# Layer 3 of a four-layer convolution net: two kinds of products move to GpSimd, a Gelu buffer changes its tag, and spectra move between pixel tiles

## The chip, the core and the metric

The kernel runs on one core of a Trainium2 chip. The core has TensorE (PE, matmuls; its weight loads are listed apart as PEld), VectorE (DVE), ScalarE (ACT), GpSimd (POOL) and SyncE (SP, which here only issues DMAs). The metric is the device time of the whole program in microseconds, as the median of several runs.

## The reference

The input is 4 images of 48 channels and 256 x 256 pixels, all in float32. Four layers follow each other, each as `x = x + layer(groupnorm(x))`. The first is a gated convolution with an 8 x 8 Fourier filter, the second and third are scans over rows and columns with five-wide convolutions. Only the fourth, layer 3, is touched:

```python
y = jnp.einsum('oc,bchw->bohw', w_in, x)                  # 48 -> 288 channels
yp = y.reshape(B, C2, ht, P, wt, P).transpose(0, 1, 2, 4, 3, 5)   # 8 x 8 patches
f = jnp.fft.rfft2(yp) * fft_mask[None]
yp = jnp.fft.irfft2(f, s=(P, P))
y = yp.transpose(0, 1, 2, 4, 3, 5).reshape(B, C2, H2, W2)
y = lax.conv_general_dilated(y, w_dw, ..., feature_group_count=C2)   # 3 x 3, per channel
x1, x2 = jnp.split(y, 2, axis=1)
g = jax.nn.gelu(x1, approximate=False) * x2
return jnp.einsum('oc,bchw->bohw', w_out, g)              # 144 -> 48
```

## The kernel before

**Tiles and steps.** Layer 3 works on pairs of images, a and b, in strips of 8 rows (RB = 8). There are two pairs, each with 32 strips and a tail step for the last row, so 66 steps. A strip is first normalised (`normed`, ACT), transposed (`turned`, PE), taken to the spectrum (`waves`, PE), multiplied by w_in (`spectrum`: matmuls `pz` on L1093, then the Fourier mask on VectorE, L1096 into `z` and L1101 into `zr`), and taken back to pixels (`pixels`: matmuls `pp` on L1131, copies on L1051 by ACT or VectorE into `z_a` or `z_b`).

**The 3 x 3 convolution.** The 288 channels are split: 2 x 128 wide ones (half 0 goes through the Gelu, half 1 is the other factor) and 2 x 16 last ones. It is done in four ways:

- image a, all 8 rows: nine taps as diagonal matmuls on PE (`taps`, L1171), units `a0` and `a1` of a step
- image b, lower 4 rows: the same on PE (`lower_taps`, L1187), unit `b`; its gate is L1197 (ACT) and L1199 (VectorE, `g_b`)
- image b, upper 4 rows: `begin` makes tap 0 on ACT (L1230) and the other eight on VectorE (L1235), for half 0 and then half 1. After tap 8 of half 0 comes the Gelu (L1237, ACT); after tap 8 of half 1 the product of both halves (L1239), in place in `whole[step]`
- the last 16 + 16 channels of both images: `narrow` makes each tap as an ACT product `part` (L1261) and a GpSimd sum (L1262) into `acc_m`, in two halves of 512 elements. Then `narrow_gate` takes the Gelu (L1280, ACT) into a buffer `curved[0]` and makes four products of 32 partitions x 512 elements (L1283), two for each j0.

The result is put together in `mixed`: matmuls with w_out, first of the product `whole` (L1298), then of `g_a`, `g_b` and `acc_m` (L1310, acc_m last); VectorE adds the residual into `xo` (L1322) and SyncE writes it out (L1329).

**Order.** PE, DVE, ACT and SP run in the order in which the program is written (`manual_schedule`); GpSimd's order is made by a scheduler. A step has three stages, in each of which `together` runs nine rounds of two PE units and mixes other work in: `3n` with unit a0, `3n + 1` with a1, `3n + 2` with b. VectorE's taps of image b wait in the queue `due`; `together` takes one in certain rounds: 0, 1, 3, 4, 6, and in every third stage in round 7 too. So half 1's taps 1 to 5 fall in stage 3n + 2, taps 6 to 8 and the product in the next stage 3n, then half 0's taps. The sums of the last channels wait in `coming` and are taken by `product`. `gate_few` calls `narrow_gate` in rounds 4 and 6 of stage 3n, and `store` (with `mixed`) follows in stage 3n + 1, after the copies of a1's pixels (L1051 on VectorE).

**Buffers.** All matmul results share one PSUM tag "w" with four buffers, so each new `pp`, `pz`, `pd` or `po` takes the place of the fourth before it and waits for its readers. In SBUF the pool `io` has two buffers per tag: `gl` (Gelu results of 1024 elements: units a0, lower_gate, and curved[0]) and `xo` (residual sums).

**Before stage 3n + 2** stands, word for word:

```python
                wave(n + 1, "AA")
                product()
                lower(n, 1, 0, "AA")
                product()
                lower(n, 1, 8, "AA")
                product()
                spectra(n + 1, 0)
```

`lower(n, 1, q0, ...)` makes half 1's pixels of image b in two tiles of eight patches' width (q0 = 0 and 8) and calls `begin` after the second. `spectra(n + 1, 0)` makes the next step's spectrum of half 0 in four parts, each with its own PSUM buffer, a group of matmuls (L1093) and one VectorE instruction (L1096).

Of the kernel before, what the change touches and what calls it, by code (L numbers as in the profile page):

```python
# [9 lines left out]
F32 = mybir.dt.float32  # L10
AF = mybir.ActivationFunctionType
ALU = mybir.AluOpType
# [21 lines left out]
class Net:  # L34
# [901 lines left out]
    def layer3(self, x, scs):  # L936
# [6 lines left out]
        nc, tc, W, H, NQ, HD = self.nc, self.tc, self.W, self.H, self.NQ, HID3  # L943
# [4 lines left out]
        with ExitStack() as st:  # L948
            pool = lambda name, bufs, **k: st.enter_context(tc.tile_pool(name=name, bufs=bufs, **k))
            wp, inp, wz = pool("w3", 1), pool("in3", 1), pool("z3", 1)  # L950
            io, mid = pool("io3", 2), pool("mid3", 1)
            ps_w = pool("ps3w", 4, space=PSUM)
            st.enter_context(tc.manual_schedule(engines=FIXED | {mybir.EngineType.SP}))
            HR = RB // 2
# [129 lines left out]
            def spectrum(xf, k, q0, n):  # L1084

                m = NM if k == 0 else NM + 2 * NR
                pz = ps_w.tile([128, 2, MM], F32, name="pz", tag="w")[:, :, 0 : n * m].rearrange(
                    "p b (q c) -> p b q c", c=m
                )
                for q in range(n):  # L1090
                    for b in range(2):
                        s = slice(64 * b, 64 * b + C)
                        nc.tensor.matmul(  # L1093
                            pz[:, b, q, :], xf[s, q0 + q, :], wi[s, NM * k : NM * k + m], start=True, stop=True
                        )
                nc.vector.tensor_tensor(  # L1096
                    zs[k][:, q0 : q0 + n].rearrange("p q b c -> p b q c"), pz[:, :, :, 0:NM],
                    mask[:, :, :, NM * k : NM * k + NM].to_broadcast([128, 2, n, NM]), ALU.mult,
                )
                if k:  # L1100
                    nc.vector.tensor_tensor(  # L1101
                        zr[:, q0 : q0 + n].rearrange("p q (c b) -> p b q c", b=2), pz[:, :, :, NM:],
                        mask[:, :, :, 2 * NM :].to_broadcast([128, 2, n, 2 * NR]), ALU.mult,
                    )
# [117 lines left out]
            whole, full, due, begun = {}, set(), [], {}  # L1222

            def begin(step, half):


                g, rows = f"b{half}", 1 if tail(step) else HR
                at = lambda t: zt[g][:, t // 3 : t // 3 + rows, t % 3 : t % 3 + W]
                acc = mid.tile([128, HR, W], F32, name=f"acc{half}", tag=f"acc{half}", bufs=2 - half)[:, 0:rows]
                nc.scalar.activation(acc, at(0), AF.Identity, bias=none, scale=wd[:, half, 0:1])  # L1230
                if half == 0:
                    whole[step] = acc

                def tap(t):
                    nc.vector.scalar_tensor_tensor(acc, at(t), wd[:, half, t : t + 1], acc, ALU.mult, ALU.add)  # L1235
                    if t == 8 and half == 0:
                        nc.scalar.activation(acc, acc, AF.Gelu)  # L1237
                    if t == 8 and half == 1:
                        nc.vector.tensor_tensor(whole[step], whole[step], acc, ALU.mult)  # L1239
                        full.add(step)  # L1240

                due.extend(((step, half), lambda t=t: tap(t)) for t in range(1, 9))

            few, coming, curved = {}, [], [None]
# [22 lines left out]
            def product(last=False):  # L1267
                while coming:
                    coming.pop(0)()
                    if not last:  # L1270
                        return

            def narrow_gate(step, j0):
                if j0 == 0:
                    curved[0] = io.tile([128, HR, W], F32, name="gl", tag="gl")
                gl, acc = curved[0], few[step]
                for j0 in (j0,) if j0 == 0 or not tail(step) else ():
                    x1, x2 = slice(32 * j0, 32 * j0 + 32), slice(32 * j0 + 32, 32 * j0 + 64)
                    rows = 1 if tail(step) else HR
                    nc.scalar.activation(gl[x2, 0:rows], acc[x1, 0:rows], AF.Gelu)  # L1280
                    for j in range(1 if tail(step) else 2):
                        to, r = slice(32 * (j0 + j), 32 * (j0 + j) + 32), slice(R2 * j, min(R2 * j + R2, rows))
                        nc.vector.tensor_tensor(acc[to, r], gl[x2, r], acc[x2, r], ALU.mult)  # L1283

            def drain(step, half):

                while any(key == (step, half) for key, _ in due):
                    due.pop(0)[1]()
# [53 lines left out]
            def unit(l, step, img):  # L1342


                n, blocks = steps.index(step), (2 * l, 2 * l + 1)
                pd = None
                if img == "b":
                    if not tail(step):
                        if l == 0:
                            both[:] = [ps_w.tile([128, 2, R2, W], F32, name="pd", tag="w") for _ in range(2)]  # L1350
                        yield from lower_taps(l, blocks, both)
                else:
                    pd = ps_w.tile([128, 2, R2, W], F32, name="pd", tag="w")
                    yield from taps(step, img, int(img[1]), blocks, pd)
                if img == "a0":
                    waiting[l] = curve(step, pd)
                    return
                assert n == 0 or steps[n - 1] in out
                if img == "a1":
                    gate(step, "a", 2 * l, waiting[l], pd)  # L1360
                elif l and not tail(step):
                    lower_gate(both)

            def together(k, aside):


                going = [unit(l, *units[l][k]) for l in range(2)]
                for t in range(9):
                    for g in list(going):
                        if next(g, None) is None:  # L1370
                            going.remove(g)
                    if t in aside:
                        aside[t]()
                    if due and (t in (0, 1, 3, 4, 6) or t == 7 and k % 3 == 0):
                        due.pop(0)[1]()
                for g in going:
                    assert next(g, None) is None

            def store(n):

                if n < 0:
                    return
                drain(steps[n], 0)
                drain(steps[n], 1)
                assert steps[n] in full
                mixed(steps[n])
                out.add(steps[n])
# [23 lines left out]
            def spectra(n, k, part=slice(None)):  # L1411
                if fresh(n):
                    for q0, m in (cuts_rest if k else cuts)[part]:
                        spectrum(state["xf"], k, q0, m)

            def lower(n, half, q0, eng):
                if q0 == 0 and n:
                    drain(steps[n - 1], half)
                pixels(steps[n], f"b{half}", q0, eng)
                if q0:  # L1420
                    begin(steps[n], half)

            def gate_few(n, j0):
                if n >= 0:
                    product(True)
                    narrow_gate(steps[n], j0)
# [11 lines left out]
            for n, step in enumerate(steps):  # L1438
                pixels(step, "a0", 0, "AA")
                pixels(step, "a0", 8, "AA")  # L1440
                product()
                spectra(n, 1, slice(0, 1))
                lower(n, 0, 0, "AA")
                spectra(n, 1, slice(1, 3))
                lower(n, 0, 8, "AA")
                spectra(n, 1, slice(3, None))
                product()
                gates = {4: lambda: gate_few(n - 1, 0), 6: lambda: gate_few(n - 1, 2)}
                together(3 * n, {0: product, 1: product} | gates)

                pixels(step, "a1", 0, "DD")
                pixels(step, "a1", 8, "DD")
                pixels_rest(step, "AA")
                store(n - 1)
                narrow(step)
                if fresh(n + 2):
                    fetch(steps[n + 2])
                turn(n + 1, "AA")
                together(3 * n + 1, {t: product for t in (0, 2, 3, 5, 6, 8)})

                wave(n + 1, "AA")
                product()
                lower(n, 1, 0, "AA")
                product()
                lower(n, 1, 8, "AA")
                product()
                spectra(n + 1, 0)
                together(3 * n + 2, {t: product for t in (0, 1, 5, 7, 8)} | {3: lambda: ready(n + 2)})
            gate_few(S - 1, 0)
            gate_few(S - 1, 2)  # L1470
# [119 lines left out]
```

## Time and profile before

| | |
|---|---|
| median of 3 runs | 12826.45 us (12825.06 to 12827.79) |
| profiled execution, its own time | 12868.7 us |
| its span, first to last instruction | 12866.9 us |
| granted TensorE clock, mean | 0.98 |
| layer 3 within it | from about 8530 us, 4337 us |
| busy there: PE, DVE, ACT, POOL | 3916, 3409, 2693, 1840 us |

The profile is of one execution. Busy times are sums over instructions; a matmul's end is modelled, and a few per cent of the matmul records can be missing. "Idle before" is the time in which an engine stood still just ahead of an instruction, with the instruction that released it; "issue" means that the profile shows nothing that it waited for. In the timeline, rows merge neighbouring instructions of one kind, and the time is that from the first one's start to the last one's end. A line such as L1235 is a line of the kernel before.

### The profile page before, as it was taken

The numbers are of one execution on the slowest core, as the hardware profiler recorded it, in microseconds if no ns is written. First come the engines' busy times: TensorE is split into PE (matmuls) and PEld (weight loads), VectorE is DVE, ScalarE is ACT, GpSimd is POOL, SyncE is SP. The second block draws the span as 40 slices with busy tenths as digits, with TensorE's granted clock in tenths as the row PEclk, the third lists the DMA queues.
The fourth block names the chain that finished last, engine by engine and source line by source line (L and its number), as shares of the span: only waits on it lengthen the run. The fifth ranks groups of instructions, "written<-read, shape, count | busy, mean of one in ns | idle before, by whom it ended". The sixth has DMA issues, their size and how long they took to land. (4 is left out here: it accounts for less than half of the span.)

```text
span 12866.9 us, 411493 instructions
## 1 busy us (share of the span) xinstructions
PE 11899.8 (92%) x190576; PEld 7862.7 (61%) x190576; DVE 7874.5 (61%) x11132; ACT 4696.2 (36%) x5761; POOL 3162.7 (25%) x2017
## 2 busy tenths in 40 slices
PE   2999999999999999999999999989999998999998
PEld 0333333335777777777777777766666666666665
DVE  6777777775333333563333335668878777777787
ACT  1444444443223200002233000026666666666665
POOL 0001001110000001550000003544444444444444
PEclk9999999999999999999999999999999999999999
DMA  7222222224765786897755977941111111111110
GB/s 177 56 55 58 54 56 59 56 54 88 150 138 155 166 160 143 206 213 153 147 140 149 178 153 166 228 97 28 28 28 28 26 23 30 26 25 28 28 28 21
DMA packets 1170307, 1223.68 MB, mean 95 GB/s; under 512 B 1027668, under 2 KB 1031756, under 8 KB 1107724
## 3 DMA queue, kind: packets, MB, share of 16 engines
q1 hardware_dynamic: 1066052, 623.85, 26.4%
q0 software_dynamic: 87488, 445.55, 12.0%
q10 hardware_dynamic: 15048, 127.96, 5.4%
q8 instruction: 1494, 24.48, 0.8%
q14 instruction: 225, 1.84, 0.1%
HBM read 699.79 MB, written 497.42 MB: 93 GB/s over the span
## 5 line engine op out<-in xcount | busy, mean ns | idle before, releaser
L682 PE MATMUL acc<-line,w_down 96*96 96x256 f32 x12240 | 2661.1, 379 | 14.6 <-ACT line L780 4.9
L1262 POOL TENSOR_TENSOR acc_m<-acc_m,part 128x512 f32<-128x512 f32 (+1 forms) x1040 | 1827.0, 1777 | 2453.3 <-ACT part L1261 2452.6
L682 PEld LDWEIGHTS acc<-line,w_down 96*96 96x96 f32 x12240 | 1989.7, 163 | 671.3 <-DVE line L824 11.5
L1235 DVE SCALAR_TENSOR_TENSOR acc<-z_b,wd,acc 128x1024 f32<-128x1024 f32 (+1 forms) x1056 | 1816.2, 1720 | 40.9 <-ACT acc L1230 11.8
L313 PE MATMUL pd<-main,diag 32*32 32x512 f32 x36864 | 1432.4, 623 | 71.0 <-issue 66.9
L1171 PE MATMUL pd<-z_a,diag 32*32 32x512 f32 x37152 | 1318.4, 596 | 52.3 <-issue 46.3
L682 PE MATMUL acc<-line,w_right 96*96 96x256 f32 x6120 | 1340.4, 380 | 23.2 <-DVE line L862 11.5
L682 PE MATMUL acc<-line,w_left 96*96 96x256 f32 x6120 | 1337.7, 379 | 9.9 <-DVE line L903 7.5
L350 DVE SCALAR_TENSOR_TENSOR acc<-rest,wd,acc 128x1024 f32<-128x1024 f32 x1024 | 1256.4, 1284 | 128.3 <-ACT acc L344 128.1
L682 PEld LDWEIGHTS acc<-line,w_right 96*96 96x96 f32 x6120 | 997.4, 163 | 354.5 <-DVE line L865 17.6
L682 PEld LDWEIGHTS acc<-line,w_left 96*96 96x96 f32 x6120 | 995.4, 163 | 338.5 <-DVE line L903 16.1
L1171 PEld LDWEIGHTS pd<-z_a,diag 32*32 32x32 f32 x37152 | 792.0, 103 | 480.9 <-issue 207.7
L124 ACT ACTIVATE nrm<-nrm 96x2 f32<-96x2 f32 (+1 forms) x7 | 1.4, 203 | 2801.5 <-DVE nrm L123 2771.2
L865 DVE SCALAR_TENSOR_TENSOR line<-acc,b_right,in 96x256 f32<-96x256 f32 x1020 | 489.3, 480 | 856.6 <-PE acc L682 848.5
L789 DVE TENSOR_TENSOR line<-acc,in 96x256 f32<-96x256 f32 x1020 | 429.0, 421 | 921.3 <-PE acc L682 916.3
L313 PEld LDWEIGHTS pd<-main,diag 32*32 32x32 f32 x36864 | 504.2, 105 | 788.9 <-issue 678.9
L824 DVE SCALAR_TENSOR_TENSOR line<-acc,b_down,in 96x256 f32<-96x256 f32 x992 | 476.0, 480 | 830.5 <-PE acc L682 822.0
L1096 DVE TENSOR_TENSOR z<-pz,mask 128x768 f32<-128x768 f32 (+2 forms) x640 | 628.8, 1005 | 518.5 <-PE pz L1093 516.3
L913 POOL TENSOR_TENSOR blk<-blk,line 96x1024 f32<-96x1024 f32 x248 | 705.4, 2873 | 606.7 <-DVE line L903 606.7
L831 ACT COPY blk<-line 96x1024 f32<-96x1024 f32 (+2 forms) x264 | 479.8, 1891 | 920.4 <-DVE line L824 760.9
L903 DVE SCALAR_TENSOR_TENSOR line<-acc,b_left,in 96x256 f32<-96x256 f32 x992 | 475.6, 479 | 529.7 <-PE acc L682 529.7
L1261 ACT ACTIVATE part<-z_m,none,wd 128x512 f32<-128x512 f32 (+1 forms) x1040 | 785.9, 803 | 7.2 <-POOL acc_m L1262 7.1
(167 smaller groups left out, 13676.9 us busy)
## 6 DMA issues: line engine op xcount, KB each, us to landing
blk<-x ACTq DMA_DIRECT2D x64, 1536.0 KB, 18.2
in<-x SPq DMA_DIRECT2D x248, 384.0 KB, 10.9
dn<-line POOLq DMA_DIRECT2D x124, 768.0 KB, 9.7
rt<-line POOLq DMA_DIRECT2D x124, 768.0 KB, 10.0
in<-rt SPq DMA_DIRECT2D x124, 768.0 KB, 11.7
in<-dn SPq DMA_DIRECT2D x120, 768.0 KB, 6.7
in<-up SPq DMA_DIRECT2D x240, 384.0 KB, 11.9
up<-blk POOLq DMA_DIRECT2D x56, 1536.0 KB, 14.4
```

What stands on the lines that cost most here:

```text
L313: nc.tensor.matmul(pd[32 * j : 32 * j + 32, i], diag[s, t, :], z[s, R2 * j + t // 3 : R2 * j + t // 3 + R2, t % 3 : t % 3 + W], start=(t = ...
L350: nc.vector.scalar_tensor_tensor(to, at(t, r), wd[:, 1, t : t + 1], to, ALU.mult, ALU.add)
L682: self.nc.tensor.matmul(acc, w[:, t, :], carry[:, :, t : t + m], start=(t == 0), stop=(t == 2))
L824: nc.vector.scalar_tensor_tensor(inner(line), acc, bd, new[r], ALU.add, ALU.add)
L831: nc.scalar.copy(blk[:, :, e, lo:hi, k // 2 : k // 2 + RH], inner(ln[:, e::2])[..., lo:hi].rearrange("p h i w -> p i w h"),)
L865: nc.vector.scalar_tensor_tensor(blocks(inner(line)), blocks(acc), br, new, ALU.add, ALU.add)
L913: (nc.vector if w0 == 0 else nc.gpsimd).tensor_tensor(part, part, inner(ln[:, f::2])[..., lo:hi].rearrange("p w i h -> p i h w"), ALU.add)
L1096: nc.vector.tensor_tensor(zs[k][:, q0 : q0 + n].rearrange("p q b c -> p b q c"), pz[:, :, :, 0:NM], mask[:, :, :, NM * k : NM * k + NM].to ...
L1171: nc.tensor.matmul(pd[32 * j : 32 * j + 32, i, 0:n, :], diag[s, half, t, :], zt[g][s, R2 * j + t // 3 : R2 * j + t // 3 + n, t % 3 : t % 3 ...
L1235: nc.vector.scalar_tensor_tensor(acc, at(t), wd[:, half, t : t + 1], acc, ALU.mult, ALU.add)
L1261: nc.scalar.activation(part, half(at(t), r), AF.Identity, bias=none[0:n], scale=wd[0:n, 2, t : t + 1])
L1262: nc.gpsimd.tensor_tensor(half(acc, r), half(acc, r), part, ALU.add)
```

## The change

Five edits, all in layer 3:

1. `narrow_gate` takes its Gelu buffer from the tag `xo` instead of `gl` (same size, same pool, two buffers).
2. Of its four products, those with j = 1 run on GpSimd, in place on their own 32 partitions; those with j = 0 stay on VectorE.
3. Image b's product L1239 (128 x 1024) runs on GpSimd.
4. The tap in round 7 is taken in the stages 3n + 1 instead of 3n.
5. Two of the four parts of `spectra(n + 1, 0)` come between the two pixel tiles of image b's half 1, the other two stay behind.

```diff
@@ begin
                     if t == 8 and half == 1:
-                        nc.vector.tensor_tensor(whole[step], whole[step], acc, ALU.mult)
+                        nc.gpsimd.tensor_tensor(whole[step], whole[step], acc, ALU.mult)
                         full.add(step)
@@ narrow_gate
                 if j0 == 0:
-                    curved[0] = io.tile([128, HR, W], F32, name="gl", tag="gl")
+                    curved[0] = io.tile([128, HR, W], F32, name="gm", tag="xo")
...
-                        nc.vector.tensor_tensor(acc[to, r], gl[x2, r], acc[x2, r], ALU.mult)
+                        (nc.gpsimd if j else nc.vector).tensor_tensor(acc[to, r], gl[x2, r], acc[x2, r], ALU.mult)
@@ together
-                    if due and (t in (0, 1, 3, 4, 6) or t == 7 and k % 3 == 0):
+                    if due and (t in (0, 1, 3, 4, 6) or t == 7 and k % 3 == 1):
                         due.pop(0)[1]()
@@ the loop over the steps
                 lower(n, 1, 0, "AA")
+                spectra(n + 1, 0, slice(0, 2))
                 product()
                 lower(n, 1, 8, "AA")
                 product()
-                spectra(n + 1, 0)
+                spectra(n + 1, 0, slice(2, None))
```

In the instruction order of the changed program GpSimd runs, in each step, the sixteen sums L1262, then the two gates L1283, then the product L1239. The order of ACT is the same as before in the steps after the first; VectorE has two gates and no product left in stage 3n, and six taps in a row ahead of g_a (L1218) instead of five. From L1465 on, the changed kernel's lines stand one further down.

## The prediction

> **What bounds the kernel now.** I read the page first, then the waits of layer 3 (8700 to 12700 us), then the timeline and the chain of one of its steps. Layer 3 runs from about 8530 us to the end in 66 steps, some 66 us each; no line of the change is executed before that. From the page:
>
> ```profile
> PE 11899.8 (92%) x190576; PEld 7862.7 (61%) x190576; DVE 7874.5 (61%) x11132; ACT 4696.2 (36%) x5761; POOL 3162.7 (25%) x2017
> L1262 POOL TENSOR_TENSOR acc_m<-acc_m,part 128x512 f32<-128x512 f32 (+1 forms) x1040 | 1827.0, 1777 | 2453.3 <-ACT part L1261 2452.6
> L1235 DVE SCALAR_TENSOR_TENSOR acc<-z_b,wd,acc 128x1024 f32<-128x1024 f32 (+1 forms) x1056 | 1816.2, 1720 | 40.9 <-ACT acc L1230 11.8
> ```
>
> TensorE is nearly full, so a gain can only come out of its idle time. The waits of layer 3 say where that is; the columns are who waits for whom, total us, times, longest:
>
> ```profile
> PE pp L1131 <- issue: 92.1, 80, 1.9
> PE pp L1131 <- DVE g_b L1199: 83.0, 58, 2.1
> PE po L1298 <- ACT gl L1212: 71.5, 57, 2.0
> ACT gl L1212 <- DVE acc_m L1283: 175.8, 57, 3.4
> ```
>
> The window holds some 60 steps, so a step loses 1.4 us to VectorE's g_b, 1.2 us to the second Gelu of unit a0 (which itself waits for the narrow gates to give back a gl buffer), and 1.5 us in which TensorE has nothing that it waits for. All its idle time comes to some 5.8 us a step, which is the ceiling. One step's timeline, first VectorE and GpSimd around the output product, then TensorE and VectorE around image b:
>
> ```profile
> 11163.82 6.36 DVE L1235 SCALAR_TENSOR_TENSOR acc<-z_b,wd,acc 128x1024 f32<-128x1024 f32 x3
> 11170.22 1.22 DVE L1239 TENSOR_TENSOR acc<-acc,acc 128x1024 f32<-128x1024 f32 x1
> 11171.46 1.38 DVE L1283 TENSOR_TENSOR acc_m<-gl,acc_m 32x512 f32<-32x512 f32 x2
> 11172.85 1.28 DVE L1235 SCALAR_TENSOR_TENSOR acc<-z_b,wd,acc 128x1024 f32<-128x1024 f32 x1
> 11174.16 1.39 DVE L1283 TENSOR_TENSOR acc_m<-gl,acc_m 32x512 f32<-32x512 f32 x2
> 11175.58 2.61 DVE L1235 SCALAR_TENSOR_TENSOR acc<-z_b,wd,acc 128x1024 f32<-128x1024 f32 x2
> 11178.11 2.48 DVE L1051 COPY z_a<-pp 128x512 f32<-128x512 f32 x4
> ...
> 11163.38 5.72 POOL L1262 TENSOR_TENSOR acc_m<-acc_m,part 128x512 f32<-128x512 f32 x3 [6.69 <-ACT part L1261]
> 11189.11 4.14 POOL L1262 TENSOR_TENSOR acc_m<-acc_m,part 128x512 f32<-128x512 f32 x2 [20.00 <-ACT part L1261]
> ```
> ```profile
> 11204.66 0.69 PE L1131 MATMUL pp<-c_inv,z 64*64 64x64 f32 x29 [1.29 <-issue]
> 11205.27 3.84 PE L1093 MATMUL pz<-wi,xf 48*128 48x128 f32 x64
> 11209.05 9.76 PE L1187 MATMUL pd<-z_b,diag 32*32 32x512 f32 x288
> 11218.73 2.10 PE L1131 MATMUL pp<-c_inv,z 64*64 64x64 f32 x128
> ...
> 11206.49 4.62 DVE L1096 TENSOR_TENSOR z<-pz,mask 128x1024 f32<-128x1024 f32 x4 [5.57 <-PE pz L1093]
> 11211.02 9.84 DVE L1235 SCALAR_TENSOR_TENSOR acc<-z_b,wd,acc 128x1024 f32<-128x1024 f32 x5
> 11220.89 2.46 DVE L1199 TENSOR_TENSOR g_b<-gl,pd 64x1024 f32<-64x1024 f32 x2
> ```
>
> See two things. A tap (L1235) takes 1.28 us while GpSimd is idle and 2.1 us beside it. And GpSimd stands idle for 20 us just where the product and the gates are made.
>
> **What the Trainium skill says.** "SBUF — State Buffer", section Who interferes with whom: a VectorE instruction with two SBUF inputs and a GpSimd instruction that reads SBUF exclude each other for the whole instruction; one with at most one SBUF input doesn't. The trace agrees: three taps and three GpSimd sums fill 11163.38 to 11170.18, 6.8 us, or 2.2 us a pair; so a 512-wide GpSimd sum, 1.27 us by itself, holds a tap up by 2.2 - 1.28 = 0.9 us. "GPSIMD Engine Reference", section Performance versus the Vector engine: a two-input operation there takes about twice VectorE's time (2048 wide: 4497 against 2293 ns). The trace agrees for 512 (1.27 us; VectorE's gate of that width 0.69). "Runtime: NRT & Kernel Launch", section Instruction fetch mechanics: instructions come in blocks of 256, mostly hidden. Here it isn't hidden: counted in the trace, TensorE's stops without a wait lie 512 of its instructions apart, 1.3 to 1.9 us each, in the stretches of short matmuls.
>
> **The change part by part**, per step, with t = 0 at L1298's start (11176.75).
>
> *1. Gelu buffer from the tag xo.* L1212's second Gelu no longer waits for the gates: it starts about -4.2, not -1.1. The xo buffers are free: the output that used one left a step ago, and the next xo that takes gm's buffer comes after the gates. TensorE is ready at -1.2 (end of L1150), so 1.2 us would come free if nothing else were late. What is late next is part 2.
>
> *2. Product and half the gates on GpSimd.* In the compiled order GpSimd does gate, gate, product: the product stands last. Its time is not in the trace. From L1262's 256- and 512-wide forms (0.71 and 1.27 us) 1024 wide gives 0.71 + 3 x 0.55 = 2.4 us, of which 2.0 hold the port; the upper bound is L913's 2.87 us at that width. VectorE loses 1.22 (product), 1.38 (two gates) and, through part 4, one tap, 1.3: 3.9 us. But all that remains there has two SBUF inputs, and GpSimd's three pieces hold the port 0.9 + 0.9 + 2.0 = 3.8 us in just these 7 us. Played through: gate at VectorE from -6.5 to -5.85, gate at GpSimd to -4.9, tap to -3.6, gate at GpSimd to -2.7, gate at VectorE to -2.0, product to 0.0, tap to 1.3; then z_a's copies (PSUM to SBUF, not held up) from 1.3, against 1.36 before. The product is readable at +0.2, so L1298 moves from 0 to +0.2; but the second half of L1310 waits for the bank that z_a's second copy frees (2.6 before), and this stays. Gain 0.1 us. If the product takes 2.87, the copies slip 0.5: loss 0.5. If GpSimd gets the port first each time, 0.1 to 0.2. If 32-partition gates did not hold the port, copies and L1298 would come 1.1 us earlier: gain 1.1. I take 0.1.
>
> *3. Two spectra between image b's pixel tiles.* The four z products (1.16 us each) now begin after the first pixel tile, in the 5.57 us that VectorE sits idle. Before, the last z ends 1.9 us after TensorE's last pz (11211.1 against 11209.1); with two left it ends one z later than that pz, 1.2: 0.8 us earlier. The five taps follow (L1230 on ACT is done 0.4 to 0.8 us before them), in the same alternation with six sums, and fall 0.2 us better: g_b starts 1.0 us earlier. It cannot come earlier than ACT's Gelu, 1.03 us after the taps' end; then TensorE (2.1 + 1.1 us of pp and pz against 1.1 + 2.46 us) waits 0.3. So 1.4 becomes 0.4: gain 1.0 us; bounds 0.3 (if ACT's later copies hold the taps) and 1.1.
> Besides, where the instruction stop falls in the second pixel tile, up to 1.9 us of pz now runs before it instead of after, while the block is under way. Over 59 steps, limited by each stop's length, that is some 0.6 us in the mean. But the next block then has short matmuls in front of it and can stop in turn for about half of that. I take 0.3; bounds -0.3 and 1.3.
>
> *4. One tap from stage 3n to 3n+1.* Its relief is in part 2. There VectorE idles 4.2 us before g_a, and the tap with one more sum costs 2.2. ACT's L1237 comes 2.2 us later and the xf copy behind it at about t = 21.7, where the first half of pf is finished at 21.5 in the median step: nothing there, up to 0.9 us in steps without a stop. I take a loss of 0.1, bounds 0 and 0.6.
>
> Sum: 0.1 + 1.0 + 0.3 - 0.1 = 1.3 us over 62 full steps, about 80 us. The profiled execution took 12868.7 us (span 12866.9); it would take 12789. The median shown is 42 us lower, 12826.45, so 12746.
>
> **Rivals.**
> - *Only the earlier g_b, and half of it given back*: the product costs as L913 (-0.5) and fetch stops return in full; 0.5 x 62 = 30 us, 12796. For it: GpSimd and VectorE would then be busy almost without a gap from -6.5 to 1.8. Against: L913's tiles are strided, these are not.
> - *Slower: the product on GpSimd is what L1298 waits for.* Place: t = -6.5 to 2. If two taps get in ahead of the product, or GpSimd needs about 0.5 us more per instruction with its waits on two other engines, L1298 starts at +1.5 and the copies at 2.5, so TensorE loses 1.2 us; with part 3 held to 0.5 by ACT's in-order queue it is 0.7 x 62 = 43 us more: 12870. It decides once the product ends more than 1.3 us later than I have it. For it: the product stands last in GpSimd's order, and L1298 reads it first. Against: all sums in the trace start within 0.2 us of what they wait for.
> - *The port isn't the limit*: 32-partition gates pass each other, L1298 starts at -1.2 and the copies early; 2.3 x 62 = 143 us: 12684. Against: L1262 shows full exclusion.
> - *That it does nothing*: two of four parts could cancel to within 0.2% (26 us), which is what a measurement of this kernel can tell from no change.
>
> **How the numbers follow.** Forecast 0.58, half given back 0.16, slower 0.14, port free 0.08, no change 0.04. Half given back lies on the 26 us bound, so I split it: faster 0.58 + 0.08 + 0.09 = 0.75; the same 0.07 + 0.04 + 0.02 of the slower case's mild end = 0.13; slower 0.12. The range runs from a gain of 2.5 us a step, with the port free or with parts 2 and 3 at their better bounds together (12670), to none (12830); it leaves out the slower case, 0.12, and some 0.05 at the other end.
>
> **What would show it.** Right: L1212 no longer waits for L1283; PE's wait for g_b falls from 83 to some 25 us; L1239 on POOL has a median of 2.4 to 3.5 us and ends beside L1298's start; z_a's copies stay near 1.3 us after it; stops on L1131 shrink, with new ones in L1187. Wrong: L1298 waits for POOL more than 1.2 us a step, or g_b's wait stays above 1 us.

## The result and the profile after

The changed kernel takes 12938.99 us (median of 4 runs, 12923.88 to 12946.48), the kernel before 12827.12 (4 runs, 12825.06 to 12832.5). The ratio is 1.008, with a 95% interval of 1.0068 to 1.0092: slower, where 80 us less was forecast. The profiled execution of the changed kernel has a span of 12944.7 us, against 12866.9; of these 78 us, layer 3 holds 77 (4337 to 4414 us from 8530 us on). The profiled execution of before is 42 us above its median and that of the changed kernel 7 us, so the profiles show 78 of the 112 us between the medians.

From the page of the changed kernel, the engines and the sums of the last channels on GpSimd:

```profile
PE 11963.8 (92%) x190576; PEld 7921.6 (61%) x190576; DVE 8071.7 (62%) x10938; ACT 4696.1 (36%) x5761; POOL 3646.3 (28%) x2211
L1262 POOL TENSOR_TENSOR acc_m<-acc_m,part 128x512 f32<-128x512 f32 (+1 forms) x1040 | 1888.1, 1836 | 1981.2 <-ACT part L1261 1980.5
```

Two things are odd. VectorE lost 194 instructions and is busy 197 us longer. TensorE has the same 190576 matmuls and is busy 64 us longer: either its work was done more slowly, or it stands in a different place. Its waits in layer 3 (8700 to 12770 us, which holds as many waits for g_b as the stretch shown of before, 58; who waits for whom, total us, times, longest):

```profile
PE pp L1131 <- DVE g_b L1199: 131.8, 58, 2.6
PE po L1298 <- POOL acc L1239: 103.7, 57, 11.8
PE pp L1131 <- issue: 50.9, 54, 1.9
```

The wait for the Gelu is gone, and L1298 waits for GpSimd's product instead; the stops without a wait fell from 92.1 to 50.9 us; and the wait for g_b, which was to fall to some 25 us, rose from 83.0 to 131.8. One step's timeline shows what became of image b. First VectorE:

```profile
10975.82 1.21 DVE L1096 TENSOR_TENSOR z<-pz,mask 128x1024 f32<-128x1024 f32 x1
10977.76 2.35 DVE L1096 TENSOR_TENSOR z<-pz,mask 128x1024 f32<-128x1024 f32 x2 [0.72 <-PE pz L1093]
10980.03 11.20 DVE L1235 SCALAR_TENSOR_TENSOR acc<-z_b,wd,acc 128x1024 f32<-128x1024 f32 x5
10991.26 2.46 DVE L1199 TENSOR_TENSOR g_b<-gl,pd 64x1024 f32<-64x1024 f32 x2
```

GpSimd in the same step, image b's sums and then the output product:

```profile
10975.94 1.27 POOL L1262 TENSOR_TENSOR acc_m<-acc_m,part 128x512 f32<-128x512 f32 x1 [1.13 <-ACT part L1261]
10979.98 5.73 POOL L1262 TENSOR_TENSOR acc_m<-acc_m,part 128x512 f32<-128x512 f32 x3 [2.76 <-ACT part L1261]
10986.04 6.32 POOL L1262 TENSOR_TENSOR acc_m<-acc_m,part 128x512 f32<-128x512 f32 x3 [0.33 <-ACT part L1261]
...
11010.70 3.99 POOL L1283 TENSOR_TENSOR acc_m<-gm,acc_m 32x512 f32<-32x512 f32 x2 [1.17 <-ACT gm L1280]
11014.76 2.69 POOL L1239 TENSOR_TENSOR acc<-acc,acc 128x1024 f32<-128x1024 f32 x1
```

And TensorE:

```profile
10978.53 9.75 PE L1187 MATMUL pd<-z_b,diag 32*32 32x512 f32 x288
10988.22 2.09 PE L1131 MATMUL pp<-c_inv,z 64*64 64x64 f32 x128
10990.24 1.09 PE L1093 MATMUL pz<-wi,xf 48*128 48x160 f32 x12
10993.87 1.16 PE L1131 MATMUL pp<-c_inv,z 64*64 64x64 f32 x64 [2.54 <-DVE g_b L1199]
10994.96 3.57 PE L1093 MATMUL pz<-wi,xf 48*128 48x160 f32 x24
10998.46 1.98 PE L1131 MATMUL pp<-c_inv,z 64*64 64x64 f32 x64
11000.37 2.84 PE L1093 MATMUL pz<-wi,xf 48*128 48x160 f32 x28
```

VectorE's five taps stand exactly where six of GpSimd's sums stand: 11.20 us, or 2.24 a tap, where the step shown of before took 9.84. TensorE is done with `b` at 10988.28, makes two more groups and then waits 2.54 us for g_b. Then it works, but slowly. Compare a step of the same kernel where the wait was a microsecond shorter:

```profile
9818.94 1.16 PE L1131 MATMUL pp<-c_inv,z 64*64 64x64 f32 x64 [1.50 <-DVE g_b L1199]
9820.03 1.90 PE L1093 MATMUL pz<-wi,xf 48*128 48x160 f32 x24
9821.86 1.16 PE L1131 MATMUL pp<-c_inv,z 64*64 64x64 f32 x64
9822.95 2.17 PE L1093 MATMUL pz<-wi,xf 48*128 48x160 f32 x28
```

The same 24 matmuls take 1.90 there and 3.57 above. The windows name the cause, in the column after the busy times of PE, PEld, DVE, ACT and POOL, the granted clock (then the DMA share and GB/s). First the stretch behind the short wait, then layer 3 as a whole in the changed kernel and in the kernel before:

```profile
9818.50:9825.50 7.00, 6.56 (x194) 5.92 (x206) 5.28 (x10) 4.42 (x8) 1.46 (x2) 1.00 0.01 2
8530.00:12944.00 4414.00, 3981.24 (x114053) 2789.10 (x114052) 3602.30 (x3254) 2686.05 (x4051) 2315.02 (x1249) 0.96 0.14 26
8530.00:12867.00 4337.00, 3916.31 (x114238) 2733.81 (x114238) 3408.76 (x3460) 2693.29 (x4062) 1840.15 (x1066) 0.97 0.15 27
```

And the stretch behind the long wait:

```profile
10993.50:11003.50 10.00, 9.63 (x188) 8.79 (x196) 5.21 (x10) 4.13 (x6) 0.66 (x1) 0.66 0.01 3
```

The clock was 1.00 behind the short wait and 0.66 behind the long one. So "busy" hid the loss: slow matmuls count as busy time. The clock records of the trace (full or half speed, nothing between) add up, from 8530 us to the end, to 217 us at half speed before and 383 after. These 166 us more lose about 83 us, if TensorE had work throughout, which is more than the 77 us that layer 3 grew.

### The profile page after: what moved, and what is told of

The parts are those of the page before. It is cut to its first block, busy times and chain, and to the rows that moved or that the text cites. A ratio compares the mean times of both kernels' runs of the same rounds, so it can differ in the third digit from the quotient of the medians.

```text
span 12944.7 us, 411929 instructions
## 1 busy us (share of the span) xinstructions
PE 11963.8 (92%) x190576; PEld 7921.6 (61%) x190576; DVE 8071.7 (62%) x10938; ACT 4696.1 (36%) x5761; POOL 3646.3 (28%) x2211
## 5 line engine op out<-in xcount | busy, mean ns | idle before, releaser
L1262 POOL TENSOR_TENSOR acc_m<-acc_m,part 128x512 f32<-128x512 f32 (+1 forms) x1040 | 1888.1, 1836 | 1981.2 <-ACT part L1261 1980.5
L1235 DVE SCALAR_TENSOR_TENSOR acc<-z_b,wd,acc 128x1024 f32<-128x1024 f32 (+1 forms) x1056 | 2117.6, 2005 | 41.1 <-ACT acc L1230 12.0
L1131 PE MATMUL pp<-c_inv,z 64*64 64x64 f32 x32768 | 632.7, 230 | 197.8 <-DVE g_b L1199 140.9
```

What stands on the lines that cost most here:

```text
L1131: nc.tensor.matmul(pp[64 * c : 64 * c + 64, l, q, :], z[f, q0 + q, b, 64 * c : 64 * c + 64], self.inv1[f, :], start=True, stop=True,)
L1262: nc.gpsimd.tensor_tensor(half(acc, r), half(acc, r), part, ALU.add)
```

## The experiments

Three theories stood against each other. **C**, the clock: the split of the spectra (edit 5) makes g_b late, TensorE's longer wait halves its clock, and that is the loss. **P**, the port: what moved to GpSimd (edits 2 and 3) shuts VectorE out, and edits 1 to 4 are the loss. Further on its milder form is called **G**: GpSimd's gates and product cost VectorE more than they take off it, whatever the clock does. Ratios are against the kernel before on the same chip, with 95% intervals.

### Which edit loses the time

`a_no_split` is the changed kernel without edit 5; `b_split_only` is the kernel before with edit 5 alone:

```diff
                 lower(n, 1, 0, "AA")
+                spectra(n + 1, 0, slice(0, 2))
                 product()
                 lower(n, 1, 8, "AA")
                 product()
-                spectra(n + 1, 0)
+                spectra(n + 1, 0, slice(2, None))
```

> The changed kernel with edit 5 alone undone: the four spectra stand together again behind image b's pixel tiles. Theory C (clock): the loss comes from the wait for g_b, which the split made longer (2.3 us a step against 1.4), long enough for TensorE's clock to be halved after it; without the split the wait is back near 1.4 us, the time at half clock in layer 3 falls from 321 us to about 150, and the time is 12800 to 12830. Theory P (port): the loss comes from the product and gates on GpSimd, which L1298 waits for; it stays without the split, and the time is 12900 or more, with the half-clock time still above 250 us.

> The kernel before with edit 5 alone: two spectra between the pixel tiles. Theory C: the five taps ahead of g_b take about 11 us instead of 9.8, because GpSimd's sums now all fall beside them; the wait for g_b is above 2 us, the half-clock time is near 300 us and the time 12880 to 12940. Theory P: the split as such gains, as forecast: the wait for g_b falls below 1 us and the time is 12740 to 12790.

`b_split_only` took 12966.69 us, 1.0091 (1.0075 to 1.0108): the split alone costs what the whole change costs (C's time was too low: the times expected here and in the next two sections count from 12827, and the kernel before took 12855.64 on this chip). Its wait for g_b:

```profile
PE pp L1131 <- DVE g_b L1199: 131.6, 56, 2.6
```

And two of the waits of `a_no_split`, in the same stretch (8700 to 12600 us):

```profile
PE po L1298 <- POOL acc L1239: 92.3, 57, 11.8
...
PE pp L1131 <- DVE g_b L1199: 81.0, 55, 2.2
```

With the split the wait for g_b is 131.6 us, without it 81.0, whatever else is in the kernel; the half-clock time goes with it (298 and 184 us in this stretch). But `a_no_split` took 12915.17, 1.0044 (1.0025 to 1.0063). As a time this is in P's range, as a ratio it lies between C (no loss) and P (0.57% or more): C is right on the split, and edits 1 to 4 aren't free either. The last experiments take these apart.

### Is it the wait or the clock?

`a_warm2` leaves the late g_b as it is and gives TensorE something to do: the group of 12 matmuls ahead of the wait (the expectation counts six) is made three times into the same bank, which repeats part of the computation with the same values.

```diff
-                for q in range(n):
+                for q in [*range(n)] * times:
...
-                spectra(n, 1, slice(0, 1))
+                spectra(n, 1, slice(0, 1), 3)
```

> The changed kernel with the first group of pz matmuls of half 1 (six matmuls with their weights, 1.1 us) made three times over into the same bank, with the same values, so that TensorE works through most of its wait for g_b. No result changes and nothing else waits for less. Theory C: the half-clock time falls below 150 us, the stage from g_b to unit a0 falls from 7.7 us to 6.1 to 6.4 in the mean, and the time falls by 60 to 110 us to 12830 to 12880, though TensorE has 2.2 us more work a step. Theory P, or any in which the clock is a side effect: no gain, 12930 to 13000.

It took 12896.65, 1.0031 (1.0018 to 1.0044), where the changed kernel has 1.008: more work, less time. The line of the wait:

```profile
PE pp L1131 <- DVE g_b L1199: 39.6, 50, 1.0
```

g_b isn't earlier: it starts 2.98 us after the end of `b`'s taps, as in the changed kernel (2.99, medians). Yet the half-clock stretches that begin within 6 us of g_b's start add up to 208 us in the changed kernel and to none here, and the stretch from g_b's end to the first taps of a0 goes from 7.67 to 6.26 us a step (means). That the wait halves the clock is thereby shown, and not just that it comes with it. Of the 1.4 us, 0.77 stay in the step's period; stops in front of L1150 and L1072, which grew from 11.0 to 25.6 and from 7.6 to 20.8 us (8700 to 12600 us of both), take part of the rest back, and the half clock between L1298 and a1's taps grew from 0.67 to 1.17 us a step. Whether the added instructions bring these about was not tried. From 8700 to 12600 us the half-clock time fell from 317 to 147 us, to about the 150 that C expected; what is left lies elsewhere in the step.

### Why g_b is late

If the cause is that all sums of GpSimd fall beside the five taps, taking two of them away from there should bring g_b back. `a_sums_moved` takes the products that feed them out of stage 3n + 2 and puts them in among the pixels of image b's half 0, ahead of the next stage 3n, so that these sums are made later; `b_sums_moved` does that to the kernel before:

```diff
                 lower(n, 0, 0, "AA")
+                product()
                 spectra(n, 1, slice(1, 3))
+                product()
                 lower(n, 0, 8, "AA")
...
-                together(3 * n + 2, {t: product for t in (0, 1, 5, 7, 8)} | {3: lambda: ready(n + 2)})
+                together(3 * n + 2, {t: product for t in (5, 7, 8)} | {3: lambda: ready(n + 2)})
```

> The changed kernel with two of the sixteen sums of a step taken from stage 3n+2 (rounds 0 and 1, beside image b's taps) to the pixel tiles ahead of stage 3n, where VectorE works from PSUM. Theory C with the collision of sums and taps as its cause: the five taps take about 9 us, g_b is 1.5 to 2 us earlier, the wait for g_b falls to 0.4 to 0.8 us, the half-clock time below 150 us, and the time is 12730 to 12800. If the taps' length is not set by the sums beside them, the wait stays near 2.3 us and the time within 20 us of 12939.

> The kernel before with two sums a step moved from image b's taps to the pixel tiles ahead of stage 3n, and nothing else. Theory C: the five taps fall from 9.8 to about 8.5 us, the wait for g_b from 1.4 to 0.4 us, the half-clock time from 200 to 130 us or less, and the time by 0.4 to 0.7%. If the sums gain only together with the split, the time stays within 0.2% of before's.

12791.55, 0.9952 (0.9935 to 0.9968), and 12779.88, 0.9951 (0.9936 to 0.9965): both faster than before. The five taps fell from 11.22 to 9.40 us and from 9.82 to 9.24 (medians; about 9 and 8.5 were expected), and g_b starts 1.17 and 1.03 us after `b`'s taps. VectorE's taps and GpSimd's sums in one step of `a_sums_moved`:

```profile
11050.98 9.40 DVE L1235 SCALAR_TENSOR_TENSOR acc<-z_b,wd,acc 128x1024 f32<-128x1024 f32 x5
...
11050.93 1.28 POOL L1262 TENSOR_TENSOR acc_m<-acc_m,part 128x512 f32<-128x512 f32 x1 [2.65 <-ACT part L1261]
11055.58 5.94 POOL L1262 TENSOR_TENSOR acc_m<-acc_m,part 128x512 f32<-128x512 f32 x3 [3.36 <-ACT part L1261]
11063.83 1.27 POOL L1262 TENSOR_TENSOR acc_m<-acc_m,part 128x512 f32<-128x512 f32 x1 [2.31 <-ACT part L1261]
11066.31 2.51 POOL L1262 TENSOR_TENSOR acc_m<-acc_m,part 128x512 f32<-128x512 f32 x2 [1.20 <-ACT part L1261]
```

Four sums stand beside the taps here, where the changed kernel had six. The two that left come behind the taps, where VectorE's products read PSUM, and take their own 1.26 to 1.27 us. In the kernel before, five sums became three. Two of TensorE's waits in `a_sums_moved`:

```profile
PE po L1298 <- POOL acc L1239: 111.1, 60, 9.7
...
PE pp L1131 <- DVE g_b L1199: 32.2, 53, 1.5
```

The wait for g_b is a quarter of what it was, and no half clock follows it within 6 us. From 8700 to 12600 us the half-clock time is 136.5 us, below the 150 expected. What remains is 1.8 us a step in front of L1298, for GpSimd, and 1.1 us of half clock a step between L1298 and a1's taps. `a_no_split_sums` (edits 1 to 4 and the moved sums) asks whether the split is then still worth anything:

> The changed kernel without the split and with the two moved sums. Theory C: the split cost only through the sums that it brought beside the taps; with the sums moved it is worth what was forecast, so without it the time is 0.2 to 0.5% above that of the same version with the split (which was 0.5% below before's), that is 0 to 0.3% below before's. If the split is of no use even so, the two are alike.

12823.95, 0.9978 (0.997 to 0.9985), against 0.9952 with the split (on another chip, each against the kernel before there): with its sums out of the way the split does gain, 0.26%.

### What edits 1 to 4 are worth

`b_gl_tap` has edits 1 and 4 alone, `b_gl_only` edit 1, `b_tap_only` edit 4:

```diff
-                    curved[0] = io.tile([128, HR, W], F32, name="gl", tag="gl")
+                    curved[0] = io.tile([128, HR, W], F32, name="gm", tag="xo")
```
```diff
-                    if due and (t in (0, 1, 3, 4, 6) or t == 7 and k % 3 == 0):
+                    if due and (t in (0, 1, 3, 4, 6) or t == 7 and k % 3 == 1):
```

> The kernel before with edits 1 and 4 alone: the Gelu buffer from the tag xo and the tap of round 7 one stage later; product and all gates stay on VectorE. Theory G (GpSimd's pieces cost VectorE more than they take off it, since they hold the shared port for 0.9, 0.9 and 2.0 us against 0.69, 0.69 and 1.22): without them z_a's copies begin about 1.3 us earlier than before and L1298 waits for nothing; the period falls by 0.8 to 1.3 us and the time is 0.3 to 0.6% below before's. If edits 1 and 4 are themselves what makes the version without the split 0.4% slower, as through the sixth tap ahead of g_a, it is 0 to 0.4% above.

> The kernel before with edit 1 alone. L1298's wait for the second Gelu goes (1.2 us a step), but the second half of L1310 still waits for z_a's second copy, which VectorE reaches no sooner: the time is 0 to 0.2% below before's. If the wait for the Gelu were what set the step, it would be 0.5% below.

> The kernel before with edit 4 alone. z_a's copies come 1.3 us earlier, but L1298 still waits for the second Gelu behind the gates; only the stop within L1310 goes, 0.4 to 0.6 us a step: the time is 0.1 to 0.3% below before's. If the sixth tap ahead of g_a costs as much as this, no change.

Alone neither shows a gain: 12848.53, 1.0001 (0.9992 to 1.001), and 12841.24, 0.9992 (0.9983 to 1.0). Together they give 12798.95, 0.9962 (0.9949 to 0.9974). The line that explains it is in the waits of `b_gl_only`:

```profile
PE po L1310 <- DVE z_a L1051: 63.5, 56, 2.2
```

With the Gelu early, L1298 starts when TensorE is ready (0.06 us of wait a step), and TensorE then waits 1.0 us for the bank that z_a's copies free, since VectorE still has its six taps, product and gates in front of them. With one tap taken out of that row the copies come early too, and L1310's wait is 7.9 us in all. With the tap alone, L1298 goes on waiting for the Gelu, 1.30 us a step.

`best145m` puts together what gained: edits 1, 4 and 5 and the moved sums, with the product and all gates on VectorE. `best_gates_pool` adds edit 2, `best_prod_pool` edit 3:

> Edits 1, 4 and 5 and the two moved sums, with product and gates all on VectorE. Theories C and G together: faster than all others, 0.7 to 1.1% below before's time, with z_a's copies 0.4 us or more ahead of those of the version that differs from it in the GpSimd pieces alone (0.5% below before's). If moving the product and gates to GpSimd is a gain once the sums are out of the way, it is slower than that version, 0 to 0.4% below before's.

> The fastest version so far (edits 1, 4, 5 and the two moved sums, 1.3% below before's time) with edit 2 added: the two gates with j = 1 on GpSimd. Theory G: each holds the port 0.9 us to spare VectorE 0.69, so z_a's copies come 0.3 to 0.6 us later and the time is 1.0 to 1.2% below before's. If the gates are a gain by themselves, it is 1.3% or more below.

> The same fastest version with edit 3 added: image b's product on GpSimd, all gates on VectorE. Theory G: it holds the port 2.0 us to spare VectorE 1.22, so z_a's copies come about 0.8 us later; standing alone in GpSimd's queue the product is done before TensorE wants it, so L1298 hardly waits. The time is 0.8 to 1.1% below before's. If the loss lies in the wait of L1298 behind gates and product alone, it is 1.2% or more below.

`best145m` took 12672.45, 0.9868 (0.985 to 0.9886), and so beats both kernels, by more than the 0.7 to 1.1% expected. Its VectorE in one step, from the taps ahead of g_b to z_a's copies:

```profile
11027.84 9.32 DVE L1235 SCALAR_TENSOR_TENSOR acc<-z_b,wd,acc 128x1024 f32<-128x1024 f32 x5
11037.19 2.46 DVE L1199 TENSOR_TENSOR g_b<-gl,pd 64x1024 f32<-64x1024 f32 x2
...
11054.08 1.22 DVE L1239 TENSOR_TENSOR acc<-acc,acc 128x1024 f32<-128x1024 f32 x1
11055.33 1.38 DVE L1283 TENSOR_TENSOR acc_m<-gm,acc_m 32x512 f32<-32x512 f32 x2
11056.72 1.29 DVE L1235 SCALAR_TENSOR_TENSOR acc<-z_b,wd,acc 128x1024 f32<-128x1024 f32 x1
11058.04 1.39 DVE L1283 TENSOR_TENSOR acc_m<-gm,acc_m 32x512 f32<-32x512 f32 x2
11059.46 1.28 DVE L1235 SCALAR_TENSOR_TENSOR acc<-z_b,wd,acc 128x1024 f32<-128x1024 f32 x1
11060.66 2.48 DVE L1051 COPY z_a<-pp 128x512 f32<-128x512 f32 x4
```

The same stretch in `a_sums_moved`, with product and half the gates on GpSimd:

```profile
11013.62 0.68 DVE L1283 TENSOR_TENSOR acc_m<-gm,acc_m 32x512 f32<-32x512 f32 x1
11014.32 2.20 DVE L1235 SCALAR_TENSOR_TENSOR acc<-z_b,wd,acc 128x1024 f32<-128x1024 f32 x1
11016.55 1.65 DVE L1283 TENSOR_TENSOR acc_m<-gm,acc_m 32x512 f32<-32x512 f32 x1
11018.23 3.25 DVE L1235 SCALAR_TENSOR_TENSOR acc<-z_b,wd,acc 128x1024 f32<-128x1024 f32 x1
11021.41 2.47 DVE L1051 COPY z_a<-pp 128x512 f32<-128x512 f32 x4
```

Here the work is shorter by three instructions and takes longer: from the first gate to the copies 7.8 us, and from the product to the copies 6.6 in `best145m`. A gate goes from 0.68 to 1.65 and the last tap to 3.25, since GpSimd's gate or product holds them up. In medians, from g_b's end to the end of z_a's second copy: 22.31 us in `best145m`, 0.49 more with the gates on GpSimd, 0.83 more with the product, 1.21 more with both. The times are 12698.05, 0.9878 (0.986 to 0.9896), and 12724.35, 0.9895 (0.988 to 0.991): the order is G's, and the second is in G's range, while the first lies between the two that were expected. But the interval of `best145m` overlaps with that of `best_gates_pool` widely and with that of `best_prod_pool` a little, so the evidence is in the copies and in what TensorE loses by them: its wait in L1310 for the bank that they free is 0.19 us a step in `best145m`, 0.57 with the gates on GpSimd and 0.94 with the product. With both, that is `a_sums_moved`, 0.9952: there L1298 waits 1.8 us for GpSimd as well.

### The steps side by side

Counted from the traces, us a step; half clock is the sum from 8700 to 12600 us:

| kernel | period | wait for g_b | wait of L1298 | five taps | half clock | time, ratio |
|---|---|---|---|---|---|---|
| before | 66.44 | 1.42 | 1.28 | 9.82 | 153.6 | 1 |
| changed | 67.78 | 2.27 | 1.71 | 11.22 | 317.4 | 1.008 |
| a_no_split | 66.95 | 1.42 | 1.54 | 9.82 | 184.3 | 1.0044 |
| b_split_only | 67.89 | 2.37 | 1.03 | 11.21 | 297.8 | 1.0091 |
| a_warm2 | 67.01 | 0.73 | 1.69 | 11.21 | 146.8 | 1.0031 |
| a_sums_moved | 65.20 | 0.58 | 1.79 | 9.40 | 136.5 | 0.9952 |
| b_sums_moved | 65.20 | 0.63 | 1.31 | 9.24 | 92.2 | 0.9951 |
| b_gl_tap | 65.29 | 1.56 | 0.05 | 9.95 | 139.9 | 0.9962 |
| best145m | 63.27 | 0.62 | 0.03 | 9.40 | 54.6 | 0.9868 |

## Why the prediction was wrong

**The step that failed is in part 3**: "The five taps follow ... in the same alternation with six sums, and fall 0.2 us better: g_b starts 1.0 us earlier." Everything ahead of it came as worked out: the last z ends 0.8 to 1.1 us earlier (mean and median; predicted 0.8, counted from L1298), and TensorE's own `b` ends 0.4 to 0.7 us earlier with it. But the alternation isn't the same, and it had five sums, not six: in 52 of 61 steps of the kernel before, five sums ran beside the five taps, in 54 of 61 of the changed kernel six. Before, the first of the six ran beside the z products, and these read PSUM and have only one operand in SBUF, so that neither holds the other up: in the step of the changed kernel above, the sum at 10975.94 took 1.27 us and the z product at 10975.82, beside it, 1.21, each its own length. The split puts two of the spectra ahead of the second tile's pixels on TensorE, and so ACT's copies of that tile, L1230 and the `part` products come later; the sums wait for `part`. Then sums and taps begin together, as the timeline shows (10979.98 and 10980.03), each tap meets a sum, and 9.82 us become 11.22. So g_b starts 0.35 us later than before, counted from L1298, and not 1.0 earlier, and the wait for it is 2.27 us a step, above the 1 us that the prediction gave as a sign of being wrong. "SBUF — State Buffer", section Who interferes with whom, in the Trainium skill, which the prediction had used for each pair, is borne out, if not quite for the whole instruction: a pair takes 2.24 us and not the 2.55 of a tap and a sum each by itself. What was not followed through was which pairs the new order makes.

**A term that the sum lacked** made a loss of it: what a wait does to the matmuls behind it. TensorE waits 0.85 us more for g_b, and the stretch behind takes 0.87 us more (6.80 to 7.67), because it runs at half clock for 3.2 us of it a step instead of 1.2. "TensorE: Matmul & The Clock Gate" in the Trainium skill, section What's actually happening, tells of the two clocks and of a free-running window of 3413 ns, and the trace agrees: nearly all half-clock stretches of the changed kernel last 3.413 or 6.827 us. Its rule in the section HAM oscillation — how this bites in real kernels, no idle gaps above some 3.4 us, is too mild here: in 40 of 62 steps the wait was over 2.3 us, the longest 2.6, and behind these the stretch, counted from its first matmul, took 7.70 us in the median instead of 6.12 at full clock; the clock fell behind 30 of the 40. What a wait of TensorE costs is thus not bounded by its own length.

**The sum.** Forecast was 1.3 us a step less; measured was 1.34 more (1.40 over the 61 steps counted next, all means). From the end of `b`'s taps to the start of a0's a step takes 13.11 us instead of 11.44: this is the longer wait and the half clock behind it. From the end of a1's taps to the start of `b`'s it takes 9.87 instead of 10.30, by fewer stops. From the end of a0's taps to the start of a1's, with L1298 between them, it takes 13.79 both times.

**Part 1** held: L1212 no longer waits for L1283 and its second Gelu starts 4.63 us before L1298 (predicted 4.2).

**Part 2** held in its detail. The product takes 2.68 us in the median (2.4 was taken) and ends 0.05 us before L1298, z_a's copies start 0.95 us after it (predicted 1.3), and without the split L1298 comes 0.2 us later behind g_b than before, as forecast. What it missed is that this near-zero was a gain spent: edits 1 and 4 without GpSimd are worth 0.38%. The rival in which L1298 waits for the product names a wait that is there, 1.7 us a step, above the 1.2 that the prediction gave as a sign of being wrong. But it took the place of the wait for the Gelu, and the stretch from a0's taps to a1's is as long as before; so it isn't what made this kernel slower than the kernel before. It is part of what GpSimd's pieces cost against `best145m`.

**Part 3's stops** went as said, and further: on L1131 from 1.54 to 0.81 us a step. TensorE's idle time stayed at 5.96 us a step (5.84 before), as the wait for g_b and the one of L1298 took up what they gave.

**Part 4** was taken as a loss of 0.1, bounds 0 and 0.6. Edit 4 alone shows no loss in the time. The stretch of a1's taps, where the sixth tap ahead of g_a falls, takes 11.31 us in the mean before, 11.46 in `b_gl_tap`, 11.48 in the changed kernel, 11.50 in `b_tap_only` and 11.75 in `a_no_split`, which is within the bounds. Parts 1, 2 and 4 together were to come to nothing, and `a_no_split`, which has these alone, lost 0.44%. Its profile shows 0.44 us a step more in a1's taps and 0.12 between a0's taps and a1's; why its a1 takes longer than that of the other kernels with the moved tap was not tried, and stays open.

## What to carry to other kernels

Before moving work past a wait of TensorE, work out not only how long the wait becomes but whether it stops the matmuls long enough to halve the clock: a microsecond more of waiting cost two here, and filling the wait with useless matmuls gained time. Work given to GpSimd cost VectorE nothing here beside products that read PSUM; beside its two-operand work in SBUF the pairs that a new order makes have to be played through one by one, upstream as well, and the cheapest change can be to move part of GpSimd's work to where VectorE reads PSUM, even if that is later. Two waits that end at nearly the same time have to be removed together, so an edit that does nothing alone isn't thereby worthless.

## What was not expected of the hardware

A wait of 2.3 to 2.6 us between dense matmuls was enough to halve the clock in 30 of 40 steps of the changed kernel, and one of 1.3 to 1.7 us mostly wasn't (7 of 32 in it and the kernel before). At half clock a group of 24 matmuls took 3.57 us instead of 1.90.

A GpSimd instruction beside a VectorE instruction with two SBUF operands cost VectorE more here than the same work would have cost it: product and two gates take 2.60 us on VectorE, and on GpSimd they made the copies behind them 1.21 us later than with all of it on VectorE.
